# First batch of an attention layer: where token operands live, and when the second set of weights is fetched

## The chip, the cores and the metric

The kernel runs on one core of one Trainium2 chip. The metric is the device time of one execution in microseconds (us); before the change the median of 3 runs was 2967.15 us (2965.55 to 2972.99). One further execution was recorded by the hardware profiler. Its engines are called PE (TensorE, matrix products), DVE (VectorE), ACT (ScalarE), POOL (GpSimd) and SP (SyncE, which here only issues DMA transfers).

## The reference

The layer is attention with a conditional normalization, followed by a short causal convolution along the tokens whose four taps per feature are the conditioning vectors. Sizes are 4 batches, 1024 tokens, 1024 features, 16 heads of 64.

```
scale, shift = split(emb @ W_emb + b_emb)
xn  = rms_norm(x, g_norm) * (1 + scale) + shift
qkv = xn @ W_qkv                      # 1024 x 1024 by 1024 x 3072, per batch
q, k = rms_norm(q, g_q), rms_norm(k, g_k)
o   = softmax(q k^T / 8) v            # 16 heads
x   = x + o + o @ W_out
x   = x + causal_conv(x, taps = cond) + conv_b
```

All of it is in float32. What the change touches is the product `xn @ W_qkv` of the first batch, and how its operands are made.

## The kernel before, in words

**The product.** `xn @ W_qkv` is computed with seven block products in place of eight. A batch's tokens are cut into two halves, the features into two halves, and the columns of W_qkv belong to two pairs of heads at a time; such a group of two pairs is a *double* (class `Double`, four per batch, `ND` = 16 in all, numbered n). The left operands are places in a list of eight: `A11, A12, S2, S1, S4, S3, A22, A21`, where S1 = A21 + A22, S2 = S1 - A11, S3 = A11 - A21, S4 = A12 - S2. The right operands are blocks of W_qkv (for the products P1, P2, P3) or differences of blocks T1 to T4 (for P5, P6, P7, P4). A product has four *pieces*, one for each tile t of 128 tokens of a half; a piece is four matmuls of 128 x 128 by 128 x 384 (`piece`, L560 to L567), so that a double has `NPR` = 28 pieces. `PRODUCTS` (L503) is their order: P1 and P2 mixed for tiles 0, 1 and then 2, 3, and then P6, P7, P4, P5 and P3 with four tiles each. DVE or ACT empties each piece's PSUM buffer (L577 to L588); there are three such buffers, and the transposes below use them too.

**Token operands.** For the operands, tokens have to be transposed, normalized and modulated by scale and shift. A *chunk* (class `Chunk`, L250) does this for 128 features of each half (k, four of them) and for a quarter of the tokens (q: tiles 0, 1 of each half, or tiles 2, 3): four PE transposes for each of two columns c (L301), modulates on ACT or DVE into the chunk's tile r (`modulate`, L243 to L248), four sums and differences on DVE (`combine`, L309, L317), and a store of the first seven places into a DRAM scratch array `scrA` (L319). The chunk tile is 8 x 256 floats per partition. Its tag "r" has two buffers; three chunks of the first batch are put in pairs of buffers of another tag, "sp". A chunk that reuses a buffer waits until the store of the chunk before it has landed. Every double reads its operands back from `scrA` (`load_a`, L538 to L546; a tile of 512 KB for each place and quarter, four buffers). Only P1 and P2 of the first double have operands made for them at once, without scratch, by `direct` (L548 to L554).

**Weights.** A double's weights are fetched by `load_w` (L522) into three buffers; `WEIGHTS` (L510) says at which piece, counted from the double's first, each load is issued. The differences T1 to T4 are computed once per group of columns d, by class `Weights` (L469): for each k twelve loads of 64 KB (L484) into eight buffers of the tag "ob", four subtractions (L499, on POOL for d = 0, on DVE afterwards), four stores into `scrB` (L500), from which `load_w` reads. In the first batch, the loads for group d + 1 are issued during double d at pieces 7, 12, 17 and 22; the subtractions for d = 1 are due 5.0 us later on the planner's clock.

**Order.** Each engine works through a list in a fixed order; PE, DVE, ACT and POOL in the order in which the program writes them, SP likewise. The program writes in a planned time: `tick` moves a clock by the cost written down for each PE step, `defer(delay, key, step)` puts a step off until that clock has come so far, `defer_quiet` avoids a stretch of softmax work, and `need(key)` brings a step forward because its result is used now. So a due time only settles the place in the lists; on the chip an instruction waits for its data and for its buffers, with all behind it on its engine. On SP, each DMA also waits for the completion of the one issued eight before.

**The start.** The embedding product comes first. Then the first batch's tokens of tiles 0 to 3 of both feature halves are scaled, `direct` makes A11 and A12 of quarter 0, and the loop below runs the first double. In it `scale` computes squares of tiles 4 to 7 on ACT (L220) and scales them on DVE (L349); chunks 0 to 3 are quarter 0, chunks 4 to 7 quarter 1. After the first double come the *units* (class `Unit`, one for each pair of heads and half of the queries): scores (L607), copies to SBUF on ACT (L615), a running maximum on DVE (L624), the maximum over partitions on POOL (L629), subtraction on DVE (L643), exponential on ACT (L647), sums on POOL (L649), the product with v (L670), and the total (L690). The pieces of later doubles are written between a unit's steps.

```
for T in range(NPR):
    if T in (1, 2):
        doubles[0].direct(T - 1, 1)
    if T == 2:
        scale()
    if 3 <= T < 3 + KH:
        for s in range(2 * T - 6, 2 * T - 4):
            for c in range(2):
                chunks[0, s].transposes(c)
    run(piece(T))
```

Of the kernel before, what the change touches and what calls it, by code (L numbers as in the profile page):

```python
# [15 lines left out]
P = 128  # L16
# [5 lines left out]
def kernel(  # L22
# [218 lines left out]
    combining = []  # L241

    def modulate(dst, src, b, j, vector=False):  # L243
        s, t = gain[:, j, b : b + 1], mod[:, NJ + j, b : b + 1]
        if vector:
            nc.vector.tensor_scalar(dst, src, s, t, ALU.mult, ALU.add)
        else:
            nc.scalar.activation(dst, src, AF.Identity, bias=t, scale=s)  # L248

    class Chunk:  # L250
# [31 lines left out]
        def transposes(self, c):  # L282
            b, k, q = self.b, self.k, self.q
            need("xg", self.name)
            if c == 0:
                if len(combining) == 2:
                    need("r", *combining.pop(0))
                combining.append((b, q, k))
                if b == 0 and (q, k) in ((0, 1), (0, 3), (1, 1)):
                    rs = [  # L290
                        apool.tile([P, KH, QN], F32, tag="sp", name=f"r_{self.name}_{i}", bufs=9) for i in range(2)
                    ]
                    self.r = lambda i: rs[i // KH][:, i % KH, :]
                    self.stores = ((rs[0], 0, KH), (rs[1][:, : KH - 1, :], KH, 7))
                else:
                    r = apool.tile([P, 8, QN], F32, tag="r", name=f"r_{self.name}", bufs=2)
                    self.r = lambda i: r[:, i, :]
                    self.stores = ((r[:, :7, :], 0, 7),)
            tp = ps_m.tile([P, 2, QN], F32, tag="m", name=f"xtp_{self.name}_{c}")
            for i in range(4):  # L300
                nc.tensor.transpose(tp[:, i // 2, i % 2 * P : (i % 2 + 1) * P], self.source(c, i), ident)  # L301
            tick(0.45)
            for h in range(2):
                place = ((A11, A21), (A12, A22))[c][h]
                modulate(self.r(place), tp[:, h, :], b, k + c * KH, b == 0 and c == 1)
            if c == 1:
                defer_quiet(1.2, ("r", b, q, k), self.combine)

        def combine(self):  # L309
            r = self.r  # L310
            for place, (p0, p1, op) in {
                S1: (A21, A22, ALU.add),
                S2: (S1, A11, ALU.subtract),
                S3: (A11, A21, ALU.subtract),
                S4: (A12, S2, ALU.subtract),
            }.items():
                nc.vector.tensor_tensor(r(place), r(p0), r(p1), op)  # L317
            for src, i0, i1 in self.stores:
                nc.sync.dma_start(scrA[self.b][self.q][:, i0:i1, self.k, :], src)  # L319
# [149 lines left out]
    class Weights:  # L469
# [6 lines left out]
        def load(self):  # L476
# [8 lines left out]
            if d:  # L485
                if d > 1:
                    defer_gap(5.0, ("B", d), 2.5, self.combine)
                else:
                    defer_quiet(5.0, ("B", d), self.combine)

# [17 lines left out]
    NPR = len(PRODUCTS)  # L508

    WEIGHTS = {"P1": -8, "P2": -4, "P6": 0, "P7": 6, "P4": 8, "P5": 12, "P3": 16}  # L510
    TIME = 2.65

    class Double:
        def __init__(self, n):
# [3 lines left out]
            for pr in self.pairs:  # L518
                pr.begin()
            self.w, self.a, self.u2, self.u3 = {}, {}, {}, {}  # L520

        def load_w(self, name):  # L522
# [15 lines left out]
        def load_a(self, i):  # L538

            _, place, t = PRODUCTS[2 * i]  # L540
            if (place, t // 2) in self.a:
                return
            for k in range(KH):
                need("r", self.b, t // 2, k)
            a = self.a[place, t // 2] = self.tile_a(place, t // 2)
# [14 lines left out]
        def piece(self, i):  # L560

            name, place, t = PRODUCTS[i]
            px, py = self.pairs
            pm = ps_m.tile([P, 512], F32, tag="m", name=f"pqkv_{self.n}_{name}_{t}")[:, :W3]
            w, a = self.w[name], self.a[place, t // 2]
            for k in range(KH):
                nc.tensor.matmul(  # L567
                    pm,
                    a[:, k, t % 2 * P : (t % 2 + 1) * P],
                    w[:, k, :],  # L570
# [294 lines left out]
    LATER = ((0, 0), (4, 0))  # L865
    GAP = 6.5
    outs, norms, chunks, weights, doubles = {}, {}, {}, {}, {}
    NB = 2 * NJ
# [4 lines left out]
    def piece(T):  # L873
# [8 lines left out]
        for m in (n, n + 1):  # L882
            for name, at in WEIGHTS.items():
                if m == 0:
                    at = max(at, 5) if at >= 0 else NPR
                if m < ND and at + (m - n) * NPR == i:
# [11 lines left out]
        if n < ND:  # L898
# [18 lines left out]

            if b == 0 and d + 1 < PB and i % 5 == 2 and i > 5 and i < 24:
                free(lambda: Weights(d + 1, i // 5 - 1).load())
            pieces.append((TIME, lambda: doubles[n].piece(i)))  # L920
# [94 lines left out]
    doubles[0] = Double(0)  # L1015
    doubles[0].load_w("P1")
    doubles[0].load_w("P2")
    scale = first_tokens(1)
    for k in range(KH):
# [8 lines left out]
    for T in range(NPR):  # L1028
        if T in (1, 2):
            doubles[0].direct(T - 1, 1)  # L1030
        if T == 2:
            scale()
        if 3 <= T < 3 + KH:
            for s in range(2 * T - 6, 2 * T - 4):
                for c in range(2):
                    chunks[0, s].transposes(c)
# [87 lines left out]
```

## Time and profile before

The profiled execution took 2966.98 us, of which 2965.2 us are the profiler's span, from which every time below is counted.

| what | us |
|---|---|
| profiled execution | 2966.98 |
| its span | 2965.2 |
| PE busy in the span | 2830.4 (95%) |
| DVE, ACT, POOL busy | 2234.6, 1694.0, 1401.2 |
| PE busy in 0 to 170 (the start and the first double) | 132.28 |
| PE busy in 170 to 217 | 40.70 of 47 |
| PE busy in 217 to 260 | 42.54 of 43 |
| PE busy in 260 to 2965 | 2614.85 of 2705 |
| DMA engines' busy share in 0 to 170, and after 260 | 0.83, 0.42 |

Busy time is the time in which an engine has an instruction under way. A timeline lists instructions of one engine in order of time and merges neighbours of the same kind: start, duration of the group, engine, line of the program, operation, result and operands with their shapes, the number of records (an `x` and a count), and in brackets how long the engine was idle before and who released it. Each float32 matmul leaves two records, and a piece eight. SPq is the queue in which SP issues DMAs; the time of such a row is the issuing and not the transfer.

### The profile page before, as it was taken

To read this page: it belongs to the slowest core of one execution; us is meant where nothing else is said; L and a number is where in the kernel's file an instruction comes from. 1 tells how busy PE (TensorE), PEld (TensorE's weight loads), DVE (VectorE), ACT (ScalarE), POOL (GpSimd) and SP (SyncE) were. 2 spreads that over 40 slices of the span, in tenths; PEclk is the share of its full clock that TensorE was granted. 3 is DMA by queue.
4 is the path that set the end of the run, shared out by engine and by line. 5 is a ranking of instruction groups with operands and counts; after the bars stand their busy time and mean duration, and the time that the engine had idled before them with its cause. 6 is when DMAs were issued, how large, how long until landed. Compare 5 with 4: busy or idle time off the path is not lost. (4 is left out here: it accounts for less than half of the span.)

```text
span 2965.2 us, 32084 instructions
## 1 busy us (share of the span) xinstructions
PE 2830.4 (95%) x10601; PEld 1335.5 (45%) x10601; DVE 2234.6 (75%) x2563; ACT 1694.0 (57%) x2233; POOL 1401.2 (47%) x574
## 2 busy tenths in 40 slices
PE   7789988999999999999999999999999999999899
PEld 3444444444444444444444444444444444443344
DVE  3368877887868777787877877878877878777863
ACT  3145667775656666665564666765565656555432
POOL 2035554456645544445545544535555555553420
PEclk9899999999999999999999999999999999999999
DMA  8854555543333445543433444543343333323333
GB/s 274 280 176 150 160 177 167 186 136 120 102 108 121 152 138 174 177 136 110 147 110 102 140 146 151 182 151 101 123 139 114 104 111 110 111 79 107 110 96 114
DMA packets 401661, 414.51 MB, mean 140 GB/s; under 512 B 40480, under 2 KB 331608, under 8 KB 401496
## 3 DMA queue, kind: packets, MB, share of 16 engines
q1 hardware_dynamic: 401496, 412.46, 44.4%
q8 instruction: 85, 1.39, 0.2%
q14 instruction: 80, 0.66, 0.1%
HBM read 336.88 MB, written 75.48 MB: 139 GB/s over the span
## 5 line engine op out<-in xcount | busy, mean ns | idle before, releaser
L567 PE MATMUL pqkv_P<-w_P,a 128*128 128x384 f32 x3584 | 1223.2, 494 | 36.2 <-issue 9.0
L649 POOL TENSOR_TENSOR sum<-sum,sp 128x1024 f32<-128x1024 f32 x384 | 974.1, 2537 | 60.2 <-ACT sp L647 34.0
L567 PEld LDWEIGHTS pqkv_P<-w_P,a 128*128 128x128 f32 x3584 | 669.1, 192 | 517.0 <-issue 79.5
L615 ACT COPY sp<-s 128x1024 f32<-128x1024 f32 x512 | 510.7, 1015 | 460.9 <-PE s L607 363.9
L624 DVE TENSOR_TENSOR mx<-mx,sp 128x1024 f32<-128x1024 f32 x384 | 526.6, 1371 | 217.7 <-ACT sp L615 193.1
L643 DVE TENSOR_TENSOR sp<-sp,mbp 128x1024 f32<-128x1024 f32 x512 | 604.8, 1212 | 33.7 <-ACT mbp L638 33.5
L629 POOL PARTITION_ALL_REDUCE mb<-mx x64 | 223.9, 3499 | 850.4 <-DVE mx L624 499.7
L647 ACT ACTIVATE sp<-sp 128x1024 f32<-128x1024 f32 x512 | 526.7, 1055 | 117.8 <-DVE sp L643 114.2
L607 PE MATMUL s<-qT,kT 64*128 64x512 f32 x2048 | 519.5, 624 | 39.4 <-ACT sp L615 23.1
L670 PE MATMUL pav<-sp,v 128*64 128x512 f32 x2048 | 472.4, 604 | 0.0
L800 PE MATMUL po<-ob,wo 128*128 128x512 f32 x992 | 436.9, 593 | 3.5 <-POOL wo L780 1.9
L832 DVE SCALAR_TENSOR_TENSOR y<-x,cols,y 128x512 f32<-128x512 f32 x192 | 320.6, 1670 | 111.3 <-ACT y L820 106.8
L649 POOL TENSOR_TENSOR sum<-sp,sp 128x1024 f32<-128x1024 f32 x64 | 151.3, 2364 | 478.4 <-ACT sp L647 288.3
L607 PEld LDWEIGHTS s<-qT,kT 64*128 64x128 f32 x2048 | 171.2, 186 | 331.4 <-issue 168.3
L670 PEld LDWEIGHTS pav<-sp,v 128*64 128x64 f32 x2048 | 136.9, 138 | 321.4 <-issue 309.5
L800 PEld LDWEIGHTS po<-ob,wo 128*128 128x128 f32 x992 | 183.2, 190 | 211.1 <-issue 202.4
L624 DVE TENSOR_TENSOR mx<-sp,sp 128x1024 f32<-128x1024 f32 x64 | 131.5, 2055 | 84.5 <-ACT sp L615 83.5
L818 ACT COPY x<-po 128x512 f32<-128x512 f32 x64 | 37.4, 585 | 227.6 <-PE po L800 205.4
L586 DVE TENSOR_TENSOR qk<-u,pqkv_P 128x256 f32<-128x256 f32 x256 | 105.6, 413 | 61.6 <-PE pqkv_P L567 59.7
L638 ACT COPY mbp<-mb 128x1024 f32<-128x1024 f32 x64 | 65.1, 1017 | 122.4 <-POOL mb L629 122.4
L441 DVE TENSOR_TENSOR qk<-qk,ms 128x1024 f32<-128x1024 f32 x64 | 123.2, 1924 | 2.2
L427 ACT ACTIVATE sq<-qk 128x512 f32<-128x512 f32 x128 | 76.1, 626 | 62.8 <-DVE qk L586 62.7
(82 smaller groups left out, 1615.2 us busy)
## 6 DMA issues: line engine op xcount, KB each, us to landing
a<-scrA SPq DMA_DIRECT2D x220, 512.0 KB
w_P<-scrB SPq DMA_DIRECT2D x64, 768.0 KB
w_P<-in_L_cond_W_qkv_dram SPq DMA_DIRECT2D x144, 256.0 KB
wo<-in_L_cond_W_out_dram SPq DMA_DIRECT2D x128, 256.0 KB
scrA<-r SPq DMA_DIRECT2D x29, 896.0 KB
xc<-in_x_dram SPq DMA_DIRECT2D x64, 256.0 KB
out_dram<-ot SPq DMA_DIRECT2D x64, 256.0 KB
rec<-scrR SPq DMA_DIRECT2D x124, 128.0 KB
```

Source lines behind the costliest of these rows:

```text
L441: nc.vector.tensor_mul(qk, qk, self.ms[g].unsqueeze(2).to_broadcast([P, 4 * HT, D]))
L567: nc.tensor.matmul(pm, a[:, k, t % 2 * P : (t % 2 + 1) * P], w[:, k, :], start=(k == 0), stop=(k == KH - 1),)
L607: nc.tensor.matmul(ps[:, h, :], pr.kT[kt // HT][h * D : (h + 1) * D, kt % HT * P : (kt % HT + 1) * P], pr.qT[self.half][h * D : (h + 1) * ...
L615: nc.scalar.copy(sp, ps)
L624: nc.vector.tensor_max(self.mx, self.mx if kt > 1 else self.sp[0], self.sp[kt])
L629: nc.gpsimd.partition_all_reduce(self.mb.rearrange("p h q -> p (h q)"), self.mx.rearrange("p h q -> p (h q)"), P, bass_isa.ReduceOp.max,)
L643: nc.vector.tensor_sub(self.sp[kt], self.sp[kt], self.mb)
L647: nc.scalar.activation(sp, sp, AF.Exp)
L649: nc.gpsimd.tensor_tensor(self.sum, self.sum if kt > 1 else self.sp[0], sp, ALU.add)
L670: nc.tensor.matmul(self.pav[h * D : (h + 1) * D, :], self.pr.v[kt // HT][:, kt % HT, h * D : (h + 1) * D], self.sp[kt][:, h, :], start=(kt ...
L800: nc.tensor.matmul(self.pm, self.w[kh][:, k % KH, :], oTs[b, k, half], start=False, stop=(k == NJ - 1),)
L832: nc.vector.scalar_tensor_tensor(self.y, self.x1[:, k : k + HN], cols[:, r : r + 1], self.y, ALU.mult, ALU.add)
```

## The change

Five things are changed, all in the first batch.

1. Each of the eight chunks has buffers of its own. Chunks (q, k) = (0, 0) and (1, 0) keep the two "r" buffers; the others are cut into tiles of 4 or 2 places and live in buffers of the tags "sp", "xg", "x" and "ob". A chunk has now one store for each tile: 7 stores for quarter 0 in place of 6, and 13 for quarter 1 in place of 5.
2. The first double reads quarter 0's operands where the chunks made them, and not from scratch. Quarter 0's stores are put off by 30 us of planned time. The order of the first double's products is P1 and P2 as before, then P6, P7 and P4 for tiles 0 and 1, then the three for tiles 2 and 3, then P5 and P3.
3. The first double's weights are loaded at other pieces: P6 at 5, P7 at 6 and P4 at 8 as before, P5 at 16 (12 before), P3 at 18 (16 before). Double 1 loads P6 at its piece 3 and not 0.
4. The blocks for the second group of weights (d = 1) are loaded at pieces 16, 19, 22 and 25 of the first double, and their subtractions are due 12 us after and not 5.
5. At the start, the loads of tiles 4 to 7 go ahead of P2's weights; `scale` runs one step earlier (T = 1), as do the chunks' transposes (from T = 2).

```diff
+    R_HOME = ("r", 8, 2)
+    R_HOMES = {(0, 1): ("sp", 4, 9), (0, 2): ("sp", 4, 9), (0, 3): ("xg", 4, 2), (1, 1): ("x", 2, 6)}
+    R_HOMES |= {(1, 2): ("ob", 2, 8), (1, 3): ("ob", 2, 8)}
...
+                tag, n, bufs = R_HOMES.get((q, k), R_HOME) if b == 0 else R_HOME
+                rs = [
+                    apool.tile([P, n, QN], F32, tag=tag, name=f"r_{self.name}_{i}", bufs=bufs) for i in range(0, 8, n)
+                ]
+                self.r = lambda i: rs[i // n][:, i % n, :]
+                self.stores = [(rs[i // n][:, : min(n, 7 - i), :], i, min(i + n, 7)) for i in range(0, 7, n)]
...
-                defer_quiet(1.2, ("r", b, q, k), self.combine)
+                defer_quiet(1.2, ("s", q, k) if b == 0 else ("r", b, q, k), self.combine)
...
+            if (self.b, self.q) == (0, 0):
+                defer(STORE, ("r", 0, 0, self.k), self.store)
+            else:
+                self.store()
...
-                    defer_quiet(5.0, ("B", d), self.combine)
+                    defer_quiet(TO_B, ("B", d), self.combine)
...
+    FIRST_PRODUCTS = PRODUCTS[:8]
+    for ts in ((0, 1), (2, 3)):
+        FIRST_PRODUCTS += [(name, a, t) for name, a in (("P6", S2), ("P7", S3), ("P4", A22)) for t in ts]
+    FIRST_PRODUCTS += PRODUCTS[20:]
...
+    WEIGHTS_FIRST = {"P6": 5, "P7": 6, "P4": 8, "P5": 16, "P3": 18}
...
-            if (place, t // 2) in self.a:
+            if (place, t // 2) in self.a or self.n == 0 and t < 2:
                 return
             for k in range(KH):
+                if self.b == 0:
+                    need("s", t // 2, k)
                 need("r", self.b, t // 2, k)
...
             for k in range(KH):
+                if a is None:
+                    need("s", 0, k)
                 nc.tensor.matmul(
                     pm,
-                    a[:, k, t % 2 * P : (t % 2 + 1) * P],
+                    (chunks[0, k].r(place) if a is None else a[:, k, :])[:, t % 2 * P : (t % 2 + 1) * P],
...
+    STORE = 30.0
+    TO_B = 12.0
+    P6_AT = 3
+    STEPS_B = ((16, 19, 22, 25), (7, 12, 17, 22))
...
                 if m == 0:
-                    at = max(at, 5) if at >= 0 else NPR
+                    at = WEIGHTS_FIRST.get(name, NPR)
+                elif m == 1 and name == "P6":
+                    at = P6_AT
...
-            if b == 0 and d + 1 < PB and i % 5 == 2 and i > 5 and i < 24:
-                free(lambda: Weights(d + 1, i // 5 - 1).load())
+            if b == 0 and d + 1 < PB and i in STEPS_B[d > 0]:
+                free(lambda: Weights(d + 1, STEPS_B[d > 0].index(i)).load())
...
     doubles[0].load_w("P1")
+    scale = first_tokens(1)
     doubles[0].load_w("P2")
-    scale = first_tokens(1)
...
-        if T == 2:
+        if T == 1:
             scale()
-        if 3 <= T < 3 + KH:
-            for s in range(2 * T - 6, 2 * T - 4):
+        if 2 <= T < 2 + KH:
+            for s in range(2 * T - 4, 2 * T - 2):
```

More of the change, by code (lines that the diff above doesn't have):

```diff
@@ L286, in transposes @@
                 if len(combining) == 2:
-                    need("r", *combining.pop(0))
+                    d, *at = combining.pop(0)
+                    need(*(("r", d, *at) if d else ("s", *at)))
                 combining.append((b, q, k))
[L289 to L298, printed above, removed]
+                tag, n, bufs = R_HOMES.get((q, k), R_HOME) if b == 0 else R_HOME
[4 more added lines that the diff above has]
+                self.stores = [(rs[i // n][:, : min(n, 7 - i), :], i, min(i + n, 7)) for i in range(0, 7, n)]
             tp = ps_m.tile([P, 2, QN], F32, tag="m", name=f"xtp_{self.name}_{c}")
@@ L317, in combine, with store @@
                 nc.vector.tensor_tensor(r(place), r(p0), r(p1), op)
+            if (self.b, self.q) == (0, 0):
+                defer(STORE, ("r", 0, 0, self.k), self.store)
+            else:
+                self.store()
+        def store(self):
             for src, i0, i1 in self.stores:
@@ L520, in __init__ @@
             self.w, self.a, self.u2, self.u3 = {}, {}, {}, {}
+            self.products = PRODUCTS if n else FIRST_PRODUCTS
         def load_w(self, name):
@@ L538, in load_a @@
         def load_a(self, i):
-            _, place, t = PRODUCTS[2 * i]
-            if (place, t // 2) in self.a:
+            _, place, t = self.products[2 * i]
+            if (place, t // 2) in self.a or self.n == 0 and t < 2:
                 return
             for k in range(KH):
+                if self.b == 0:
+                    need("s", t // 2, k)
                 need("r", self.b, t // 2, k)
@@ L560, in piece @@
         def piece(self, i):
-            name, place, t = PRODUCTS[i]
+            name, place, t = self.products[i]
             px, py = self.pairs
             pm = ps_m.tile([P, 512], F32, tag="m", name=f"pqkv_{self.n}_{name}_{t}")[:, :W3]
-            w, a = self.w[name], self.a[place, t // 2]
+            w, a = self.w[name], self.a.get((place, t // 2))
             for k in range(KH):
+                if a is None:
+                    need("s", 0, k)
                 nc.tensor.matmul(
                     pm,
-                    a[:, k, t % 2 * P : (t % 2 + 1) * P],
+                    (chunks[0, k].r(place) if a is None else a[:, k, :])[:, t % 2 * P : (t % 2 + 1) * P],
                     w[:, k, :],
```

## The prediction

> **What bounds the kernel now.** I read the slices of the page first. PE is nine tenths busy or more from the fourth slice on (74 us each); the first three, with a lower granted clock, are where time lies open.
>
> ```profile
> PE   7789988999999999999999999999999999999899
> PEclk9899999999999999999999999999999999999999
> ```
>
> Then PE's timeline there. A product piece is 8 matmul records (four 128-row steps, two records each). Columns: start, duration, engine, line, operation, count, idle before and who ended it.
>
> ```profile
> 62.65 3.37 PE L567 MATMUL pqkv_P<-w_P,a 128*128 128x384 f32 x8
> ...
> 79.43 1.11 PE L301 MATMUL xtp<-ident,x 128*128 128x128 f32 x4 [5.65 <-ACT r L248]
> 80.33 4.75 PE L567 MATMUL pqkv_P<-w_P,a 128*128 128x384 f32 x8
> ...
> 95.87 10.75 PE L567 MATMUL pqkv_P<-w_P,a 128*128 128x384 f32 x24 [5.91 <-ACT r L248]
> 108.73 2.82 PE L567 MATMUL pqkv_P<-w_P,a 128*128 128x384 f32 x8 [2.11 <-DMA a<-scrA]
> 113.51 2.85 PE L567 MATMUL pqkv_P<-w_P,a 128*128 128x384 f32 x8 [1.96 <-DVE u L579]
> 116.68 10.56 PE L567 MATMUL pqkv_P<-w_P,a 128*128 128x384 f32 x32 [0.32 <-DMA a<-scrA]
> 131.16 7.12 PE L567 MATMUL pqkv_P<-w_P,a 128*128 128x384 f32 x16 [3.92 <-DVE u L582]
> ...
> 162.51 4.51 PE L567 MATMUL pqkv_P<-w_P,a 128*128 128x384 f32 x8 [1.11 <-issue]
> ...
> 167.29 2.75 PE L567 MATMUL pqkv_P<-w_P,a 128*128 128x384 f32 x8
> ...
> 217.15 0.81 PE L690 MATMUL tot<-sum,ones 128*32 128x256 f32 x8 [4.42 <-POOL sum L649]
> ```
>
> The reader sees: an unhindered piece is 10.56 / 4 = 2.64 us; ten of the first double's 28 pieces are done at 106.6, all at 169.97; the last 18 took 63.4 us. At 217.15 PE waits for the first unit's softmax. Third, DVE and the queue of SP:
>
> ```profile
> 78.34 0.99 DVE L246 TENSOR_SCALAR r<-xtp,mod 128x256 f32<-128x256 f32 x2 [2.95 <-DMA scrA<-r]
> 94.79 0.99 DVE L246 TENSOR_SCALAR r<-xtp,mod 128x256 f32<-128x256 f32 x2 [7.79 <-DMA scrA<-r]
> 126.05 0.56 DVE L499 TENSOR_TENSOR b<-b,b 128x384 f32<-128x384 f32 x1 [5.96 <-DMA b<-in_L_cond_W_qkv_dram]
> 128.83 1.81 DVE L499 TENSOR_TENSOR b<-b,b 128x384 f32<-128x384 f32 x3 [2.22 <-DMA b<-in_L_cond_W_qkv_dram]
> 174.43 5.21 DVE L624 TENSOR_TENSOR mx<-mx,sp 128x1024 f32<-128x1024 f32 x4
> ```
> ```profile
> 54.95 5.59 SPq L484 DMA_DIRECT2D b<-in_L_cond_W_qkv_dram  x12
> 149.00 7.27 SPq L484 DMA_DIRECT2D b<-in_L_cond_W_qkv_dram  x12
> ```
>
> So two things hold PE up: chunk operands waiting for a room until a store has landed (78, 94), and DVE standing at a combine whose weight blocks have not landed (126), which keeps it from emptying PSUM.
>
> **The change, part by part.**
>
> *Scaling earlier.* The eight squares on ACT began at 51.07; now they follow the modulates that end at 47.12: 4.0 us sooner. DVE's scaling (4.32 us) then runs 52.9 to 57.2. But the A12 transposes of quarter 1 come after it, and their two modulates (0.54 each) queue behind the scaling, to 58.3; the chunk transposes need those PSUM buffers. PE is then a piece behind, DVE, which paces this stage, 1.7 us ahead (first chunk modulate at 59.9, not 61.6).
>
> *Own rooms.* From 61.6 DVE needs until 98.6 for the eight chunks: 37.0 us, idle 0.30 + 2.95 + 1.24 + 1.50 + 7.79 = 13.8, so 23.2 of work. With no wait for stores: 23.2 + 0.7 (adds of the P2 piece that moved behind) + 1.7 for PSUM turns left = 25.6, end at 85.5. The "ob" rooms come free with the first double's scrB stores, issued by 73.7, and are first written near 79: no wait. The last P2 pieces end near 89.4, P6's first two at 94.7, where ten pieces took until 106.6: **11.9 us**. P6 to P4 of tokens 0 and 1 read the rooms, so the wait at 108.73 and five loads of 0.5 MB go.
>
> Stores: 20 instead of 11. The Trainium skill, "DMA: Bandwidth & Descriptors", section on the anatomy of one DMA, gives each about 2 us of fixed cost (for the GpSimd path); nine more, one after another, would be 18 us on the loads of P6's weights behind them, and speak against the split. Nearest row: 12 loads of 64 KB were issued in 5.59 us, 0.47 each, side by side. I take the row: 9 x 0.47 = 4 us of SP, while it waits for DVE's combines anyway. P6's weights (issued near 82.5, behind 1.8 MB of stores at the 325 GB/s of 75 to 100 us) land near 88.6, just in time; P7's, behind the next stores, near 96, 1.5 us late.
>
> *Second weights later.* DVE's eight waits for b in the first double sum to 23.7 us, and made PE wait 1.96 and 3.92. Now the first combine stands behind P4's last add, with its loads sent about 10 us before. The 18 remaining pieces cost 18 x 2.64 + 4 transposes of 0.44 = 49.3, plus P7's 1.5, plus 1.8 for one slow piece as at 162.51. Double ends at 94.7 + 52.6 = 147.3 against 169.97: **22.7 us gained**.
>
> On the slow pieces: the skill's "TensorE: Matmul & The Clock Gate", in why it matters, says a PE gap over some 3 us drops the clock to half, for 3.4 us of work. Three long gaps go: by rule 3 x 1.7 = 5.1 us, by rows (4.75, 10.75 and 7.12 against 2.64 a piece) 2.1 + 2.8 + 1.8 = 6.7, which the sum above holds. It speaks against one part: the gap of 3.9 us before 57.7 stays and more pieces follow it. By rule 1.7, by row (3.37 at 62.65) 0.7; both hidden while DVE paces. The piece at 162.51 was slow with only 0.95 and 1.11 us idle before it, which the rule doesn't foresee; so I keep 1.8.
>
> *What is late next.* The fourth block row of second weights (b_3) is now combined between the first unit's second and third running maximum; before, it was done at 159.7, ahead of the unit. Behind it on DVE stand five maxima, on which hang GpSimd's maximum, the exponentials, GpSimd's sums and PE's wait at 217.15: no slack, so every microsecond is PE's. SP reaches these loads only after P5's weights, which take the buffer that P6's last piece frees (six pieces on: P7's and P4's first two, P6's last two; 94.7 + 1.5 + 6 x 2.64 = 112.0). From there to b_3's last issue: 4 x 7.3 for b (the row at 149), 8 for ten weight DMAs (three took 2.84 at 145.6), 8 x 0.4 for stores (four took 1.57 at 129.4) + 2 for the landing that frees rooms, 1.4 for three loads of a (0.43 each) = 43.8, so 155.8; landed 1.7 later (second b wait of the fourth row, 157.95, against SP's last issue at 156.3), three combines of 0.58: 159.2. Undisturbed, the second maximum ends 5.8 us into the unit: 147.3 + 5.8 = 153.1. **Loss 6.1 us.** Ends: 2.3 (four combines, nothing late) and 15 (b at the 9.64 us that one row took). I take 6.
>
> Everything behind keeps its order on PE and DVE (P6's load of double 1, three pieces later, has 40 us to spare; from 200 to 225 the DMA engines are 7% busy). Sum: 22.7 - 6.1 = 16.6: span 2965.2 to 2948.6, that execution 2966.98 to 2950.4; the median 2967.15 is 0.17 over that execution, so the same holds for it: **2950.5**.
>
> **Rivals.**
>
> *All of it (2944).* Loads go at 5.59 per row as at 55 us: 7 us sooner, the loss is 2.3, and the double saves 1 to 2 more if no slow piece comes: 23. For: SP has fewer loads of a among them. Against: at 149 the same row took 7.27.
>
> *Late loads eat half (2959).* Rows at 9 us or P5's weights later: loss 14, gain 8. For: before, SP took 57 us for the same four rows (99.3 to 156.4), with six more loads of a and waits for PE.
>
> *Slower (2975).* The same queue: should it need more than 61 us after P6's last piece, b_3 comes over 22.7 us late and every further one is lost; at 69 us, +8. Needs more than the 57 it took before; only if stores and the backlog of quarter 0 (3.7 MB from 95 us) hold it up.
>
> *Not what it says (2962).* Rooms still wait (the "ob" rooms for scrB stores, PSUM for DVE): the 11.9 is gone. Against: SP had sent those stores by 73.7.
>
> **Numbers.** Forecast 0.45, all of it 0.2, half 0.2, not what it says 0.05, slower 0.1. About 0.3% (9 us) is what a measurement tells from no change. Faster: 0.45 + 0.2 + half of 0.2 = 0.75; within: 0.15; slower 0.1. Range 2941 to 2963 holds all but the slower case.
>
> **What would show it.** Right: no DVE wait for scrA stores; last P2 piece ended by 90; scores from about 147; a DVE wait for b between two maxima; PE's wait at tot near 10 us. Wrong: PE waiting for w_P or a between 90 and 147, or first scores after 155; the wait at tot over 25.

## The result, and the profile after

The changed kernel takes 2948.03 us (median of 6 runs, 2941.86 to 2956.63), the kernel before, run beside it, 2966.81 us (6 runs, 2963.21 to 2973.2): a ratio of 0.9934, 95% interval 0.9912 to 0.9956, or 18.8 us less. The forecast was 2950.5 us. The profiled execution took 2953.38 us, of which 2951.6 us are the span: 13.6 us under the profiled execution before.

The slices of the page for the changed kernel; one slice is 74 us:

```profile
PE   7989988999999999999999999999999999999898
PEclk9999999999999999999999999999999999999999
```

Of the first four slices only the second, 74 to 148 us, has changed, from 7 to 9: there the time has come out. The granted clock shows it too. In the table of windows, PE's busy time from 90 to 150 us has risen from 45.82 to 57.22 us of 60, at a granted clock of 0.97 where it was 0.91. From 150 to 205 us it has fallen from 51.22 to 47.01 us of 55 (0.94 after 0.97): there, something is given back.

PE's timeline of the changed kernel, with the columns as before. The program has grown by 19 lines, so that a piece is now L586, scores are L626 and the total is L709:

```profile
81.97 7.98 PE L586 MATMUL pqkv_P<-w_P,a 128*128 128x384 f32 x24
90.32 5.40 PE L586 MATMUL pqkv_P<-w_P,r 128*128 128x384 f32 x16 [0.38 <-DMA w_P<-scrB]
97.81 12.25 PE L586 MATMUL pqkv_P<-w_P,r 128*128 128x384 f32 x32 [2.09 <-DVE qk L449]
...
148.47 1.99 PE L626 MATMUL s<-qT,kT 64*128 64x512 f32 x8
...
167.81 4.31 PE L586 MATMUL pqkv_P<-w_P,a 128*128 128x384 f32 x8 [2.63 <-ACT u L596]
...
176.97 4.51 PE L586 MATMUL pqkv_P<-w_P,a 128*128 128x384 f32 x8 [4.41 <-issue]
...
200.37 0.64 PE L709 MATMUL tot<-sum,ones 128*32 128x256 f32 x8
```

Pieces whose operand is `r` read a chunk's room, those with `a` a tile read back from scratch. P2 ends at 89.95, P6's first two pieces at 95.72, and the first scores come at 148.47, where they came at 169.97: 21.5 us sooner. P7's wait of 2.09 us is put down to DVE, but its weights had been issued only at 90.93, behind eight stores of chunks; in a repeat of the same kernel the same wait (2.21 us) is put down to `w_P<-scrB`. The first total, which is where a unit's softmax shows, comes at 200.37 and not at 217.15: 16.8 us sooner. So 4.7 of the 21.5 us have gone again within the first unit: it takes 51.90 us from first scores to first total, where it took 47.18.

DVE's timeline in that unit (L643 is the running maximum, L507 the combine of weights), and the row of SP that feeds it:

```profile
152.94 1.23 DVE L643 TENSOR_TENSOR mx<-mx,sp 128x1024 f32<-128x1024 f32 x1
156.16 0.56 DVE L507 TENSOR_TENSOR b<-b,b 128x384 f32<-128x384 f32 x1 [2.00 <-DMA b<-in_L_cond_W_qkv_dram]
160.32 1.74 DVE L507 TENSOR_TENSOR b<-b,b 128x384 f32<-128x384 f32 x3 [3.60 <-DMA b<-in_L_cond_W_qkv_dram]
161.98 3.88 DVE L643 TENSOR_TENSOR mx<-mx,sp 128x1024 f32<-128x1024 f32 x3
```
```profile
149.08 7.88 SPq L492 DMA_DIRECT2D b<-in_L_cond_W_qkv_dram  x12
```

Two waits for weight blocks stand between the second and the third maximum, as the forecast had it. The third maximum could have begun at 154.3 and begins at 161.98: 7.7 us late. What this costs PE does not show as a wait at the total, though. ACT's next small step of the normalization (L444) stands behind a sum of DVE (L441) that stands behind the maxima, and ACT's copies out of PSUM stand behind that:

```profile
167.08 0.31 ACT L444 ACTIVATE ms<-ms,eps 128x16 f32<-128x16 f32 x1 [8.16 <-DVE ms L441]
167.30 0.84 ACT L596 COPY u<-pqkv_P 128x384 f32<-128x384 f32 x2
```

So PE runs out of PSUM buffers at 165.2, for 2.63 us, and again before 176.97. There the view says "issue", but the piece starts 0.1 us after DVE has emptied a buffer (176.87), behind a subtraction that had waited for the late maximum. Each of these two gaps is followed by a slow piece (4.31 and 4.51 us for 2.64), with the granted clock at 0.50 from 167.38 to 170.79 and from 177.62 to 181.03.

### The profile page after: what moved, and what is told of

Same layout as the page of the kernel before. It is cut to its first block, busy times and chain, and to the rows that moved or that the text cites. A ratio compares the mean times of both kernels' runs of the same rounds, so it can differ in the third digit from the quotient of the medians.

```text
span 2951.6 us, 32110 instructions
## 1 busy us (share of the span) xinstructions
PE 2830.6 (96%) x10601; PEld 1336.0 (45%) x10601; DVE 2228.2 (75%) x2563; ACT 1694.3 (57%) x2233; POOL 1402.3 (48%) x574
## 4 chain that ended last, share of the span: by engine, by line
PE 75%; DVE 9%; ACT 7%; POOL 3%; issue 2%; DMA 2%; SPq 1%; DVEq 0%; ACTq 0%; POOLq 0%
PE pqkv_P L586 29%; PE po L819 14%; PE pav L689 14%; PE s L626 13%; ACT sp L634 3%; DVE mx L643 2%; POOL sum L668 2%; DVE sp L662 2%; ACT sp L666 2%; DVE y L851 1%; POOL mb L648 1%; PE tot L709 1%; PE qkt L457 1%; PE otp L862 1%; PE po L805 1%
## 5 line engine op out<-in xcount | busy, mean ns | idle before, releaser
L586 PE MATMUL pqkv_P<-w_P,a 128*128 128x384 f32 x3504 | 1189.9, 492 | 27.5 <-issue 11.3
L586 PEld LDWEIGHTS pqkv_P<-w_P,a 128*128 128x128 f32 x3504 | 650.7, 191 | 493.2 <-issue 73.2
L643 DVE TENSOR_TENSOR mx<-mx,sp 128x1024 f32<-128x1024 f32 x384 | 524.5, 1366 | 223.0 <-ACT sp L634 199.1
L626 PE MATMUL s<-qT,kT 64*128 64x512 f32 x2048 | 520.3, 624 | 40.6 <-ACT sp L634 24.9
L626 PEld LDWEIGHTS s<-qT,kT 64*128 64x128 f32 x2048 | 171.3, 186 | 333.4 <-issue 167.8
L643 DVE TENSOR_TENSOR mx<-sp,sp 128x1024 f32<-128x1024 f32 x64 | 126.9, 1983 | 86.3 <-ACT sp L634 85.5
```

The costliest lines, as they stand in the source:

```text
L586: nc.tensor.matmul(pm, (chunks[0, k].r(place) if a is None else a[:, k, :])[:, t % 2 * P : (t % 2 + 1) * P], w[:, k, :], start=(k == 0), s ...
L626: nc.tensor.matmul(ps[:, h, :], pr.kT[kt // HT][h * D : (h + 1) * D, kt % HT * P : (kt % HT + 1) * P], pr.qT[self.half][h * D : (h + 1) * ...
L643: nc.vector.tensor_max(self.mx, self.mx if kt > 1 else self.sp[0], self.sp[kt])
```

## The experiments

Twelve runs were made, of ten kernels; each computes the whole layer, and each was timed beside the kernel before on one chip. The first row is the result above. The ratios are estimated from the single executions, and lie up to 0.0008 off the quotient of the two medians. First scores and first total are from the profiled execution of each, "between" is their difference.

| kernel | median (range) us | before us | ratio (95%) | first scores | first total | between |
|---|---|---|---|---|---|---|
| changed | 2948.03 (2941.86 to 2956.63) | 2966.81 | 0.9934 (0.9912 to 0.9956) | 148.47 | 200.37 | 51.90 |
| changed, again | 2949.59 (2944.65 to 2954.42) | 2969.47 | 0.9932 (0.9920 to 0.9945) | 145.72 | 196.50 | 50.78 |
| own rooms alone | 2968.36 | 2969.95 | 1.0001 (0.9991 to 1.0011) | 168.49 | 217.22 | 48.73 |
| late weights alone | 2955.25 | 2969.47 | 0.9958 (0.9945 to 0.9970) | 157.26 | 204.83 | 47.57 |
| own rooms and late weights | 2956.44 | 2969.47 | 0.9959 (0.9946 to 0.9971) | 158.53 | 205.98 | 47.45 |
| changed, quarter 0 by scratch | 2952.77 | 2969.95 | 0.9944 (0.9928 to 0.9960) | 154.11 | 201.66 | 47.55 |
| changed, weights early again | 2968.08 | 2969.95 | 0.9992 (0.9984 to 0.9999) | 166.05 | 214.79 | 48.74 |
| changed, without part 5 | 2946.44 (2944.77 to 2951.16) | 2973.19 | 0.9907 (0.9890 to 0.9923) | 145.54 | 195.35 | 49.81 |
| changed, b_3 behind the maxima | 2942.67 (2932.94 to 2944.05) | 2969.95 | 0.9903 (0.9886 to 0.9921) | 145.37 | 188.82 | 43.45 |
| the same, again | 2945.22 (2936.55 to 2946.16) | 2973.19 | 0.9898 (0.9882 to 0.9914) | 147.80 | 191.61 | 43.81 |
| the same, third time | 2945.38 (2945.0 to 2950.28) | 2968.07 | 0.9930 (0.9917 to 0.9944) | 147.81 | 191.97 | 44.16 |
| the same, `direct` first | 2943.67 | 2969.47 | 0.9913 (0.9899 to 0.9926) | 147.26 | 191.16 | 43.90 |
| b_3 behind the maxima, without part 5 | 2942.55 (2940.82 to 2944.16) | 2968.07 | 0.9917 (0.9903 to 0.9930) | 144.19 | 188.28 | 44.09 |

Two profiles of one kernel differ by up to 2.8 us in the first scores (changed: 148.47 and 145.72), so a smaller difference between two single profiles tells nothing by itself.

**Own rooms alone.** The forecast's second step gave the rooms 11.9 us. Into the kernel before, only the chunks' buffers of part 1 were put:

```diff
-                if b == 0 and (q, k) in ((0, 1), (0, 3), (1, 1)):
...
-                    r = apool.tile([P, 8, QN], F32, tag="r", name=f"r_{self.name}", bufs=2)
+                tag, n, bufs = R_HOMES.get((q, k), R_HOME) if b == 0 else R_HOME
+                rs = [
+                    apool.tile([P, n, QN], F32, tag=tag, name=f"r_{self.name}_{i}", bufs=bufs) for i in range(0, 8, n)
+                ]
...
```

> The kernel before with rooms of their own for the eight chunks and nothing else of the change: every chunk is stored at once and read back from scratch, products, weights and scaling as before. Theory (two of the waits, 2.95 and 7.79 us on DVE, are for landed stores, and they are worth 10 to 12 us of the gain): DVE shows no wait for scrA stores, the last P2 piece ends 8 to 12 us earlier than at 98.6, but the loads of a from scratch and the combines of second weights then stop PE, so that the first scores come 3 to 10 us earlier than at 170.0; median 2957 to 2964. Rival (the bound is the bytes in flight, so that a shorter wait for rooms only turns into a longer wait for loads): first scores within 2 us of 170, median within 2 us of the kernel before.

The ratio is 1.0001: nothing, as the rival said, and the first scores (168.49) lie within its 2 us. The rooms did what they should: P2 ended at 86.2, where before the chunks alone had taken until 98.6. Then came this, in PE's and DVE's timelines of this kernel:

```profile
90.78 6.81 PE L567 MATMUL pqkv_P<-w_P,a 128*128 128x384 f32 x16 [4.56 <-DMA a<-scrA]
105.96 5.17 PE L567 MATMUL pqkv_P<-w_P,a 128*128 128x384 f32 x8 [8.37 <-DMA a<-scrA]
```
```profile
107.13 0.56 DVE L499 TENSOR_TENSOR b<-b,b 128x384 f32<-128x384 f32 x1 [19.05 <-DMA b<-in_L_cond_W_qkv_dram]
```

DVE no longer waits for a room, so PE waits 12.9 us for operands that have to go out to scratch and come back; and DVE, early at its weight combine, stands there 19.05 us, where its longest wait for weights had been 6.01. The wait has moved, and the bytes through SP's queue are the same: from 86 to 100 us the DMA engines move 377 GB/s, with hardly a pause (a busy share of 1.06 in the view), where before they moved 326 at 0.91. One thing was not separated: this kernel also has 20 stores in place of 11, and rooms that keep 11 stores were not tried.

**Late weights alone.** Part 4 in the kernel before (here and below, `at` is a local name for the steps):

```diff
-                    defer_quiet(5.0, ("B", d), self.combine)
+                    defer_quiet(12.0, ("B", d), self.combine)
...
-            if b == 0 and d + 1 < PB and i % 5 == 2 and i > 5 and i < 24:
-                free(lambda: Weights(d + 1, i // 5 - 1).load())
+            at = (7, 12, 17, 22) if d else (16, 19, 22, 25)
+            if b == 0 and d + 1 < PB and i in at:
+                free(lambda: Weights(d + 1, at.index(i)).load())
```

> The kernel before with part 4 alone: the second weights' blocks are loaded at pieces 16, 19, 22 and 25 and combined 12 us after. Theory as it stands after the first four runs (SP's one queue is the bound of the start: 48 small loads for the second weights, 7 to 9 us for each row of 12, stand ahead of loads that PE needs; taking them back gave up the whole gain): the first scores come 6 to 14 us earlier than at 170.0, DVE's waits for scrA stores (2.95 and 7.79 us) stay, and with the late b_3 tot follows 50 to 52 us after: net 3 to 10 us faster, median 2960 to 2967. Rival (the waits for rooms hold DVE up first, so the weights alone bring nothing): first scores within 3 us of 170, and slower by the late b_3, 2970 to 2975.

It took 0.9958 of the time, better than the theory's upper edge. DVE still waits for chunks' stores (3.28 and 7.80 us), but the waits for weight blocks in the middle of the double are gone, and PE, once past 108.89, has no wait until the first scores at 157.26, 12.7 us sooner than before. In PE's and DVE's timelines of this kernel:

```profile
108.89 20.88 PE L567 MATMUL pqkv_P<-w_P,a 128*128 128x384 f32 x64 [2.69 <-DMA a<-scrA]
```
```profile
162.87 2.33 DVE L499 TENSOR_TENSOR b<-b,b 128x384 f32<-128x384 f32 x4
```

The second row is b_3. It is not late here, against the theory: its four combines wait for nothing, and the unit takes 47.57 us and not 50 to 52.

**Both together.** Own rooms and late weights in the kernel before:

> The kernel before with own rooms and part 4: eight rooms, stores at once, every operand of P6 to P3 read back from scratch in the old order, second weights late. Theory (rooms are worth about 10 us as soon as SP is free to send the loads of a behind the stores): first scores 150 to 157, that is 6 to 12 us earlier than with late weights alone; median 2951 to 2958. Rival (rooms are worth nothing, late weights do it): first scores within 3 us of the run with late weights alone.

The ratio is 0.9959, as for late weights alone: the rival again. PE's timeline of this kernel says why:

```profile
92.37 8.44 PE L567 MATMUL pqkv_P<-w_P,a 128*128 128x384 f32 x16 [5.46 <-DMA a<-scrA]
108.20 22.84 PE L567 MATMUL pqkv_P<-w_P,a 128*128 128x384 f32 x64 [7.40 <-DMA a<-scrA]
```

12.9 us of waiting for operands from scratch are left. In the changed kernel, which reads quarter 0 where it was made and takes its pieces first, 0.38 and 2.09 us of waiting stand in this place.

**Quarter 0 by scratch again.** From the changed kernel the direct reading was taken out, the order of products and all else kept:

```diff
-            if (self.b, self.q) == (0, 0):
+            if False:
...
-            if (place, t // 2) in self.a or self.n == 0 and t < 2:
+            if (place, t // 2) in self.a:
```

> The changed kernel, but quarter 0's operands are stored at once and read back from scratch by the first double, as quarter 1's are; rooms, order of products and weights stay. Theory (direct reading is worth the wait for the first loads of a and 2.6 MB of transfers): PE waits for a<-scrA at P6's first piece, the first scores come 2 to 6 us later than at 148.5, and the whole is 2 to 6 us slower than the changed kernel. Rival (rooms do it all): within 1.5 us. Rival (direct reading carries most of the gain): 10 us or more slower.

First scores came at 154.11, 5.6 us after those of the changed kernel's first profile, at the theory's upper edge, and 8.4 after those of its second. Before P6's first piece PE waits for operands:

```profile
97.79 7.04 PE L586 MATMUL pqkv_P<-w_P,a 128*128 128x384 f32 x16 [6.77 <-DMA scrA<-r]
```

In the median only 3 to 5 us of it are left, since the unit is shorter in turn (47.55 us between): b_3 is combined at 159.72 with nothing to wait for, though still between the second and the third maximum.

**Weights early again.** The changed kernel with the loads and combines of the second weights where they were:

```diff
-    TO_B = 12.0
+    TO_B = 5.0
...
-    STEPS_B = ((16, 19, 22, 25), (7, 12, 17, 22))
+    STEPS_B = ((7, 12, 17, 22), (7, 12, 17, 22))
```

> The changed kernel with part 4 taken back: the second weights' blocks are loaded at pieces 7, 12, 17 and 22 and combined 5 us after. Theory (DVE standing at combines whose blocks have not landed keeps PSUM full): DVE waits for b sum to 15 to 25 us before the first scores, the first scores come 5 to 10 us later than at 148.5, and as b_3 is then combined ahead of the unit, tot follows them after 47 us: net 1 to 6 us slower than the changed kernel. Rival (rooms and direct reading alone free the start, the loads' time doesn't matter): first scores within 2 us of 148.5 and, with b_3 early, the kernel 3 to 5 us faster than the changed one.

Nearly the whole gain is gone: 0.9992, 20.1 us over the changed kernel's first median and 18.5 over its second. The loss is several times what the theory allowed (1 to 6 us; first scores came 17.6 us later and not 5 to 10), and the rival falls altogether. In this kernel's timelines of PE and of SP, two rows carry it:

```profile
129.88 5.46 PE L586 MATMUL pqkv_P<-w_P,a 128*128 128x384 f32 x8 [7.32 <-DMA a<-scrA]
```
```profile
119.92 3.81 SPq L327 DMA_DIRECT2D scrA<-r  x4
123.77 1.29 SPq L563 DMA_DIRECT2D a<-scrA  x1
```

Quarter 0's stores, put off by part 2, and the loads of operands for P4 of the later tiles now stand in SP's queue behind two rows of weight blocks (8.08 and 8.75 us of issuing from 90.90 and 104.02), and the load that PE waits for is issued at 123.77. DVE's waits for blocks sum to 32.5 us in this double (23.7 in the kernel before; the theory had 15 to 25). So this kernel shows more than the loads' time alone: early loads meet stores that part 2 has put off. Early loads with stores at once were not tried in the changed kernel.

**b_3 behind the maxima.** The changed kernel with the last combine put off a little more:

```diff
-                    defer_quiet(TO_B, ("B", d), self.combine)
+                    defer_quiet(18.5 if self.k == KH - 1 else TO_B, ("B", d), self.combine)
```

> The changed kernel, with the combine of the fourth row of second weights (b_3) written behind the first unit's last running maximum instead of between the second and the third. Theory (the maxima wait for that combine, and with them the softmax chain to PE's wait at tot): the first scores start at the same time (148.5 us), the first tot comes 45 to 47 us after them and not 51.9, and the median falls by 4.5 to 6.5 us, to about 2942 to 2943.5. Rival (the 51.9 us come from slow matmul pieces and from PSUM, not from that combine): tot stays over 50 us after the first scores, median within 2 us of 2948.

> The changed kernel with the last combine of the second weights behind the first unit's maxima, once more, to tell the size of its gain from the spread between runs. Theory (the late b_3 costs 5 to 8 us): first scores to first total 43 to 45 us, median 2939 to 2945. Rival (the first run of it was a lucky one): median over 2946, within 2 us of the changed kernel's 2948.

The first of these runs lies within the theory in the median, 2942.67, with a unit shorter than it said (43.45 us). The median of the second, 2945.22, lies between its theory and its rival. DVE's timeline of the second:

```profile
152.26 5.21 DVE L643 TENSOR_TENSOR mx<-mx,sp 128x1024 f32<-128x1024 f32 x4
...
161.04 3.91 DVE L507 TENSOR_TENSOR b<-b,b 128x384 f32<-128x384 f32 x4
```

The maxima follow each other without a break, and the four combines come after them with nothing to wait for. The unit takes 43.45, 43.81 and 44.16 us in three profiles against 51.90 and 50.78 in the changed kernel: 6.6 to 8.5 us, every time. The medians of 2942.67, 2945.22 and 2945.38 against 2948.03 and 2949.59 put the gain at 3 to 7 us; where it stood beside the changed kernel on one chip, in the variant with `direct` first, it was 5.9 us (2943.67 and 2949.59). Whether the first run was a lucky one can't be told: its median is the lowest of the three by 2.6 us, but by the ratio to the kernel before the second is the best (0.9903, 0.9898, 0.9930). What the second run's rival would have, hardly any gain, does not fit the units.

**`direct` first.** In the same kernel, both `direct` calls at T = 1 ahead of the scaling:

```diff
-        if T in (1, 2):
-            doubles[0].direct(T - 1, 1)
         if T == 1:
+            doubles[0].direct(0, 1)
+            doubles[0].direct(1, 1)
             scale()
```

> The changed kernel with b_3 combined behind the maxima, and with the A12 operands of quarter 1 made ahead of the scaling of tiles 4 to 7 (both direct calls at step 1). Theory (their two modulates queue behind 5.5 us of scaling on DVE, and the chunk transposes wait for the PSUM buffers): PE's 3.0 us wait at xtd goes, P2's first piece comes 2 to 3 us sooner, but the scaling and with it the chunks come 1 us later, and DVE paces: within 2 us of the kernel with b_3 behind the maxima. Rival (PE's order paces): 3 us faster than that.

First scores at 147.26 and a median of 2943.67 lie inside the runs without this edit: as its theory had it, it does nothing that can be told.

**The changed kernel again**, beside these:

> The changed kernel as it is, on the chip of these runs, as their measure. Every theory: ratio to the kernel before 0.991 to 0.996, first scores within 3 us of 148.5, tot 50 to 54 us after.

The ratio repeats the first to 0.0002. In this profile the first total came 20.7 us sooner than before, and yet the medians are alike. Profiles hold the difference: of these 20.7 us, 16.6 are left at the eighth unit's total and 12.7 at the 63rd, in slow pieces of stages that the change does not touch.

**Part 5 taken back.** The changed kernel with the old order of the start:

```diff
-    scale = first_tokens(1)
     doubles[0].load_w("P2")
+    scale = first_tokens(1)
...
-        if T == 1:
+        if T == 2:
             scale()
-        if 2 <= T < 2 + KH:
-            for s in range(2 * T - 4, 2 * T - 2):
+        if 3 <= T < 3 + KH:
+            for s in range(2 * T - 6, 2 * T - 4):
```

> The changed kernel with part 5 taken back: the loads of tiles 4 to 7 again behind P2's weights, the scaling at T = 2, the chunks' transposes from T = 3. Theory: the squares begin 4 us later, but DVE, which paces the chunks, starts its first chunk modulate only about 1.1 us later (61.6 against 60.5), so the first scores come 1 to 2 us later than in the changed kernel (147 to 150) and the median is within 3 us of its. Rival: the transposes' place on PE matters more than DVE's start, since each chunk is now one piece later while P6's weights and rooms wait for it: first scores 5 us or more later (over 152), median over 2953.

The rival falls: first scores at 145.54, far from its 152. The median, 2946.44, is within the theory's 3 us. The first scores are sooner than the theory's 147, but within 0.2 us of the changed kernel's second profile (145.72), so that this profile alone shows no gain. PE's timeline of this kernel at the end of P2:

```profile
81.14 5.40 PE L586 MATMUL pqkv_P<-w_P,a 128*128 128x384 f32 x16 [0.34 <-DVE r L251]
87.80 10.66 PE L586 MATMUL pqkv_P<-w_P,r 128*128 128x384 f32 x32 [1.26 <-DVE ms L441]
```

When the chunks are done, two pieces of P2 are left, and three in the changed kernel (7.98 us at 81.97). The earlier scaling puts chunk transposes ahead of a piece, and the piece is then missing at the end, when nothing else hides it. It brings DVE's first chunk modulate only 0.9 us forward (60.51 against 61.38), because the scaling of eight tiles took 5.47 us in the changed kernel and 4.22 here. What costs DVE this time stands beside it on POOL. In the changed kernel, DVE's and POOL's timelines, and the eight scalings' shortest, median and longest time in ns:

```profile
54.21 5.47 DVE L357 TENSOR_SCALAR x<-x,rn 128x512 f32<-128x512 f32 x8
```
```profile
54.29 3.52 POOL L507 TENSOR_TENSOR b<-b,b 128x384 f32<-128x384 f32 x3 [1.83 <-DMA b<-in_L_cond_W_qkv_dram]
```
```profile
L357 DVE TENSOR_SCALAR x<-x,rn x8: 472/480/1223, 54.2 to 59.2; 128x512 f32<-128x512 f32 x8
```

Three of the eight, one for each of POOL's three subtractions of weights, took 1.21 to 1.22 us, the other five 0.47 to 0.49. In all fourteen profiles a scaling that ran clear of POOL took at most 0.49 us, and each one over 1.2 us ran beside a subtraction. There are three of these in seven of the eight profiles with part 5 (two in the eighth), and one or none in the six without it: the earlier scaling runs into POOL's work. No experiment moved that work.

**Without part 5, b_3 behind the maxima.** Both edits together, and the second alone on the same chip:

> Both edits that gave something taken together: the last combine of the second weights behind the first unit's maxima, and part 5 taken back. Theory (part 5 costs PE a piece's place at the end of P2 and brings DVE only 0.9 us): first scores 144 to 147, first total 43 to 45 us after them (188 to 191), median 2 to 3 us under that of the changed kernel with the first edit alone, run beside it. Rival (what part 5 did to the first scores lies within the spread): the two medians within 1.5 us of each other, or the other way round.

> The changed kernel with the last combine of the second weights behind the first unit's maxima, beside the kernel above on the same chip. Theory: first scores 145 to 148, first total 43 to 45 us after them, median 2940 to 2947; the kernel above 2 to 3 us under it. Rival: no difference to the kernel above.

2942.55 against 2945.38, 2.8 us, within what the theory gave; the slowest run of the one (2944.16) is faster than the fastest of the other (2945.0). First scores at 144.19 are the earliest of all, and again two pieces of P2 are left. PE's timeline of this kernel:

```profile
81.13 5.40 PE L586 MATMUL pqkv_P<-w_P,a 128*128 128x384 f32 x16 [0.90 <-DVE r L251]
86.69 10.56 PE L586 MATMUL pqkv_P<-w_P,r 128*128 128x384 f32 x32 [0.16 <-DMA w_P<-scrB]
99.66 5.40 PE L586 MATMUL pqkv_P<-w_P,r 128*128 128x384 f32 x16 [2.42 <-DMA w_P<-scrB]
```

The six pieces that read rooms are done at 105.06 here and at 105.16 in the kernel above, and at 106.97 to 110.06 in the six profiles that have both part 5 and the direct reading with late weights. The intervals of the two ratios (0.9903 to 0.9930, 0.9917 to 0.9944) still overlap a little, so that the gain of 2.8 us is likely and not certain. This is the version to keep: its ratio to the kernel before is 0.9917, the changed kernel's 0.9934.

## Why the prediction was right, and where it was not

**The sum held.** At the first total the forecast had 16.6 us, and the profile has 16.8: first scores 147.3 (148.47), the second loss 6 (4.7). That it is so close is partly luck: the gain came out 1.2 us smaller and the loss 1.4 us smaller, and the two errors cancel; in the second profile the first total had 20.7 us. The median is 2.5 us under the forecast, the profiled execution 3.0 over its own (2953.38 against 2950.4). Of the forecast's own signs, P2's end (89.95), the scores (148.47), DVE's wait between two maxima and the end of DVE's waits for stores all came; the wait at the total did not.

**The share of the rooms did not.** "Own rooms: 11.9 us" was worked out as if a room's wait were all that held those pieces. DVE's part of it was right to a few tenths: 25.6 us of chunk work from the first modulate, and 60.51 to 86.1 measured. But of the 11.9, the rooms alone bring none (1.0001), nor do they beside late weights (0.9959 against 0.9958). The operands go by one queue and one scratch array, and that path was as late as the rooms: 12.9 us of PE's waiting for them came in place of the 11.9. Only with the direct reading, for which the rooms are needed, is the time won; and without the late weights even that is all but lost (0.9992). Counted one after the other, late weights bring 12 to 14 us of the median (0.9958, 2955.25 against 2969.47), and parts 2, 3 and 5 on top of rooms and late weights 10 to 13 more in the first scores (158.53 to 148.47 or 145.72) and 7 to 8 in the median, since b_3 takes part of it back. Of the 10 to 13, the direct reading by itself is 5.6 to 8.4 (the kernel with quarter 0 by scratch); the other 4.4 are the new order, the other pieces for weight loads and part 5 together. Part 5 more likely costs than brings; the first two were not tried one by one. The forecast did have both edits on its path to 94.7; it credited the sum to the rooms, and would have erred by the whole 11.9 us on a change that made rooms alone.

**P6 and P7's weights.** P6 just in time (0.38 us of wait) and P7 1.5 us late (2.09): right. SP's timeline of the changed kernel in this stretch (L327 are the stores, L547 the loads of weights):

```profile
79.32 4.97 SPq L327 DMA_DIRECT2D scrA<-r  x5
84.39 0.63 SPq L547 DMA_DIRECT2D w_P<-scrB  x1
85.11 5.66 SPq L327 DMA_DIRECT2D scrA<-r  x8
90.93 1.57 SPq L547 DMA_DIRECT2D w_P<-scrB  x2
...
95.86 10.32 SPq L327 DMA_DIRECT2D scrA<-r  x7
```

The twenty stores took more of SP than the 4 us added: 20.95 us for twenty (4.97, 5.66 and 10.32) and 12.33 for the eleven before, so 8.6 more. Neither 0.47 us each (the row chosen) nor 2 us each (the figure of the Trainium skill's "DMA: Bandwidth & Descriptors", section on the anatomy of one DMA, for the GpSimd path) describes them. The three rows carry 1.84, 1.84 and 3.67 MB, that is 369, 324 and 356 GB/s, while their time per store goes from 0.71 to 1.47 us: bytes describe them better than a price per store. From 86 to 110 us the DMA engines are busy throughout (shares of 1.03 and 1.07 in the view, at 354 and 383 GB/s), so the likely reading is that SP waits for bytes sent before. It is no rate to count with elsewhere: the kernel before sent quarter 0's 3.67 MB in one row of 6.80 us. On PE's path it shows as P7's wait, 0.6 us longer than forecast.

**Later weights.** The 18 pieces took 52.75 us (95.72 to 148.47) where 52.6 were forecast, the slow piece among them: 12.25 us for four where 10.56 is unhindered, 1.7 for the 1.8 kept. It came behind a gap of 2.09 us, with the granted clock at 0.50 from 99.12 to 102.53. The rule of the Trainium skill ("TensorE: Matmul & The Clock Gate", section on HAM oscillation: gaps over some 3.4 us) does not reach that gap; behind gaps of 2.21 and 2.42 us in two other profiles no slow piece came, and the clock stayed at 1.00. Keeping it was right, though not as a sure cost: what decides is how a gap lies in time (see the last section). The piece at 162.51 in the kernel before, which the forecast could not place, comes out of the same count.

**b_3.** The place was right, and its price too small: the third maximum 7.7 us late and not 6.1. SP came to these loads at 115.25 (112.0 forecast: P6 began 1.0 later, P7's wait 0.6 longer, and the slow piece), needed 41.7 us where 43.8 were forecast, and the last block landed 3.4 us after its issue and not 1.7. One row was misread on the way: three stores, and not four, took 1.57 us at 129.4, which would have put eight of them at 4.2 us in place of 3.2. Against the unit with b_3 out of the way (43.5 to 44.2) PE loses 6.6 to 8.5 us; the 47.18 of the kernel before, used as the yardstick, was not undisturbed. And PE's wait was forecast at the total (near 10 us), where there is none: it came at PSUM, two stages earlier.

**Earlier scaling.** "PE is then a piece behind, DVE 1.7 us ahead" names both effects and weighs neither against the other. DVE's lead was 0.9 to 1.1 us: the scaling began 2.6 us sooner (54.21 against 56.84), and took 1.15 us longer where the forecast kept its 4.32. The piece behind is in the forecast's end of P2 (89.4, measured 89.95), but what P2 would have done in the old order is not: it ends at 86.54 and 86.53 without part 5, and at 88.96 to 91.03 in the eight profiles with it, 2.4 to 4.5 us later.

**The slices.** The first reading was off: slices six, seven and 38 of PE also show 8, and of the first three only the second shows a lower clock digit (in the table of windows the three have 0.95, 0.88 and 0.95). The sum does not rest on it.

**The rivals.** "All of it" (2944) does not stand for the changed kernel, but it is nearly what the b_3 edit gives: the loss at b_3 is the difference. "Late loads eat half" and "slower" needed SP to take 57 to 69 us; it took 41.7. "Not what it says" falls with DVE's waits for stores, which are all gone.

What stays open is the part of the spread behind the first unit. In eleven of the thirteen profiles, the lead over the kernel before shrinks by 1.8 to 8.0 us between the first total and the last, the 64th; in late weights alone it grows by 1.5 us, and in the first run with b_3 behind the maxima by 5.9. The kernel before, from which these leads are counted, has one profile too. The granted clock over the span goes with it (0.987 where the changed kernel took 2956.63 us, 0.994 in the run of 2932.94 us). No experiment was made on its cause.

## What to carry to other kernels

A wait for a buffer that is removed is worth nothing until the next thing that the same work needs is also in time: before counting it, follow the operand on to its reader, through the queue that carries it. Where loads for later share one queue with loads for now, moving the later ones back can be worth more than any buffer, but then look at the first consumer that stands in line behind them, and put it behind the critical work as well. A step moved forward on one engine pushes another step back on the same engine, and can run into work of another engine; both have to be costed where they surface.

## What the runs showed that was not expected

- The same eight scalings on DVE took 5.1 to 5.5 us in the eight profiles with part 5 and 3.3 to 4.4 in the six without it, and the difference goes with the number of them that ran beside a subtraction on POOL (at most 0.49 us for each clear of POOL; 1.21 to 1.27 for the long ones, every one of them beside a subtraction).
- A wait that a timeline calls "issue", or puts down to an engine that had long been done, was, in the two places read closely here, one for a buffer or a DMA.
- Gaps of about 2.1 to 2.4 us in PE's work are followed by a slow piece in some executions (after 2.09, 2.12, 2.12 and 2.19 us) and not in others of the same stage (after 2.21 and 2.42 us). The traces show what divides them. In the table of windows (length, busy time of PE, PEld, DVE, ACT and POOL, then the granted clock, DMA share and GB/s), first the changed kernel, then its repeat, then the kernel before at its piece of 162.51:

```profile
95.71:99.12 3.41, 1.32 (x5) 0.87 (x5) 1.94 (x3) 0.00 (x0) 0.00 (x0) 1.00 0.99 373
99.12:102.53 3.41, 3.41 (x7) 1.80 (x6) 0.51 (x1) 0.00 (x0) 0.00 (x0) 0.50 1.02 378
...
95.36:98.77 3.41, 1.42 (x5) 0.92 (x6) 1.76 (x3) 0.00 (x0) 0.00 (x0) 1.00 1.00 393
98.77:102.19 3.42, 3.42 (x12) 2.04 (x11) 0.55 (x1) 0.00 (x0) 0.00 (x0) 1.00 1.05 391
...
159.47:162.88 3.41, 1.36 (x7) 0.72 (x6) 3.41 (x11) 1.51 (x3) 0.00 (x0) 1.00 1.08 341
162.88:166.29 3.41, 3.41 (x7) 1.86 (x6) 1.44 (x3) 0.00 (x0) 0.00 (x0) 0.50 0.98 349
```

Within each of the fourteen traces the stretches at half clock, 183 in all, begin at multiples of 3.413 us from one another, to within 0.03 us. Between 44 and 2900 us the clock fell 166 times in all. In the 3.41 us ahead of each fall PE was idle for 1.74 us or more in sum, and no stretch at full clock with more than 2.02 us idle was followed by another at full clock; in between, both happen. So the changed kernel's gap lies in one stretch whole (2.09 us idle), a part of its repeat's longer gap lies in the stretch before (1.99 left), the 2.42 us are split into 1.59 and 0.83, and before 162.51 two short gaps add up in one stretch (2.05). This count was made on the finished traces; no run was built to try it.
